# A two-layer relational graph convolution with a layer norm: batches of three 14-tile chunks instead of single 10-tile chunks, on one core

## The chip, the cores and the metric

One core of a Trainium2 chip (trn2) runs the whole kernel. The metric is device time in microseconds (us) of one execution; the time given for a kernel is the median of several runs. One more execution is taken by the hardware profiler, and all rows, timelines and waits below are of that one. Engines are named as the profile names them: PE is TensorE, PEld its weight load, ACT is ScalarE, DVE is VectorE, POOL is GpSimd, SP is SyncE.

## The reference

There are 50,000 nodes with 128 features, 850,000 edges sorted by their destination, 16 relations and 8 bases. A layer sums the sources of all edges per destination and relation, multiplies by the relation's matrix (a mix of the bases), adds the node's own product and a bias, and applies a relu. Two layers follow each other, and the input plus the second layer's output is normalised.

```python
W = jnp.einsum('rb,bio->rio', w_comp, basis)
seg = dst.astype(jnp.int32) * N_REL + rel.astype(jnp.int32)
agg = jax.ops.segment_sum(h[src], seg, num_segments=N_ENT * N_REL)
agg = agg.reshape(N_ENT, N_REL, -1)
msg = jnp.einsum('nri,rio->no', agg, W)
out = jax.nn.relu(msg + h @ loop_w + bias)
...
h = layer(x, basis1, w_comp1, loop_w1, bias1)
h = layer(h, basis2, w_comp2, loop_w2, bias2)
return _layernorm(x + h, axis=-1)
```

## The kernel before

Edges are cut into tiles of 128, one edge per partition: 6,641 tiles in each layer. As edges are sorted by destination, a tile's edges belong to a few neighbouring nodes: the kernel allows 12 (WN). It first reads all destinations and builds, for the whole graph, the source indices `src`, the node of each edge within its tile (`key`), and the place of each tile's 12 slots within a window of 128 nodes (`slot`, `base_i`, `dist`); a flag read at the end of this phase chooses `chunked` or a slower way, `summed`, which doesn't run here.

`chunked` walks over chunks of 10 tiles (K), 665 per layer. For each tile, POOL gathers the 128 source rows by an indirect DMA (L156, called at L437) into one of six buffers of 10 tiles (`rows`). SP loads the chunk's 128-node window of the layer's input (`hw`), in layer 2 also of x (`xw`). Every fourth chunk `weights` (L347 to L374) turns the relations of 40 tiles into each edge's 8 basis weights `pm`: a compare on DVE (L364) and five matmuls (L367). DVE makes `own` (L442), which says which of the 12 slots an edge belongs to, and `hot` (L449), its product with the 8 weights. Then PE makes one matmul per tile (pa, L460): the gathered rows are the stationary operand and `hot` the moving one, 96 columns wide, so pa holds 8 x 12 sums per feature. ACT copies five tiles' sums at a time to `aT` (L467).

The rest of a chunk, `finish`, is done one chunk later. `slots` (L376) multiplies `aT` by the 8 bases in 8 matmuls (ps, L380) with `aT` stationary and the basis moving, 128 columns; ACT copies the result (L384). `nodes_of` (L387) sends the 120 slots to the window's nodes by a matmul with a 0/1 matrix `own` (pn, L394) and adds the part that belongs to this window from the chunk before, shifted (L397, L398); `kept` hands the sum on (L400). The window's own rows are transposed (`turned`, L163, copied by ACT at L165) and multiplied by `loop_w` (po, L402), the bias is added (L404, L405), and `ended` (L408) applies the relu and stores (layer 1, L411 and L412), or adds x, normalises (`normed`, L317 to L331, the last step on ACT at L330) and stores to the output.

The Tile framework orders each engine's instructions and gives them semaphores. Gathers signal eight shared semaphores in turn, so that each gather waits for the one eight before it; each also waits for the pa matmul that read its place in the buffers 60 tiles before. Each pa matmul waits for its own gather's semaphore. Tile is free to interleave pa matmuls with ps matmuls of the chunk before, and does.

Layer 2's gathers read layer 1's output H, so they begin only when all stores to it have landed.

## Time and profile before

| what | value |
|---|---|
| median of 3 runs | 19,358.97 us (19,357.04 to 19,359.93) |
| the profiled execution | 19,372.98 us, its span 19,371.2 us |
| POOL busy | 12,549.9 us in 13,290 instructions, 13,282 of them gathers |
| PE busy | 10,651.0 us in 60,630 records (an fp32 matmul leaves two) |
| DVE, ACT busy | 4,042.3 us, 3,098.8 us |
| DMA, mean busy share | 0.24 in the middle of layer 1, 0.25 in that of layer 2 |
| granted PE clock, mean | 0.711 |
| pause of the gathers between the layers | 46.26 us |

A row of the profile's groups reads: line, engine, operation, tile written <- tiles read, shape, count | busy us in total, mean ns of one | idle us of the engine just before them, and what ended most of it. "remote" and "another core or an unknown queue" stand for a wait whose releaser the trace doesn't name; this kernel has one core, so it is something of its own. "issue" means that nothing visible was waited for. A timeline row reads: start, duration, engine, line, operation, tiles, and in brackets the idle time before it and what ended it.

### The profile page before, as it was taken

To read this page: it belongs to the slowest core of one execution; us is meant where nothing else is said; L and a number is where in the kernel's file an instruction comes from. 1 tells how busy PE (TensorE), PEld (TensorE's weight loads), DVE (VectorE), ACT (ScalarE), POOL (GpSimd) and SP (SyncE) were. 2 spreads that over 40 slices of the span, in tenths; PEclk is the share of its full clock that TensorE was granted. 3 is DMA by queue.
4 is the path that set the end of the run, shared out by engine and by line. 5 is a ranking of instruction groups with operands and counts; after the bars stand their busy time and mean duration, and the time that the engine had idled before them with its cause. 6 is when DMAs were issued, how large, how long until landed. Compare 5 with 4: busy or idle time off the path is not lost.

```text
span 19371.2 us, 191086 instructions
## 1 busy us (share of the span) xinstructions
PE 10651.0 (55%) x60630; PEld 10113.3 (52%) x60630; DVE 4042.3 (21%) x11719; ACT 3098.8 (16%) x8680; POOL 12549.9 (65%) x13290
## 2 busy tenths in 40 slices
PE   4555555555555555555545555555555555555555
PEld 4555555555555555555545555555455555555555
DVE  2111111111111111111212222222222222222222
ACT  1111111111111111111111111111111111111111
POOL 6666666666666666666566666666666666666665
PEclk6767777777766777767767777777777777777777
DMA  2222222222222222222222222222222222222222
GB/s 74 61 61 61 61 61 60 61 61 60 61 61 60 61 61 61 60 60 61 57 62 65 65 65 65 65 66 65 65 65 65 65 66 65 65 65 65 65 66 58
DMA packets 961778, 1218.82 MB, mean 63 GB/s; under 512 B 275684, under 2 KB 704100, under 8 KB 960768
## 3 DMA queue, kind: packets, MB, share of 16 engines
q0 software_dynamic: 425024, 871.30, 18.2%
q1 hardware_dynamic: 525876, 333.73, 5.8%
q8 instruction: 493, 8.08, 0.2%
q14 instruction: 517, 4.24, 0.1%
q10 hardware_dynamic: 9868, 1.48, 0.1%
HBM read 1118.27 MB, written 87.16 MB: 62 GB/s over the span
## 4 chain that ended last, share of the span: by engine, by line
another core or an unknown queue 41%; PE 32%; issue 15%; ACT 6%; DVE 3%; POOL 1%; DMA 1%; ACTq 0%; POOLq 0%; DVEq 0%; SPq 0%
PE pa L460 12%; PE ps L380 9%; PE pn L394 4%; PE pn L398 2%; PE po L402 2%; ACT aT L467 2%; PE pm L367 2%; ACT o L330 1%; PE po L163 1%; POOL g L156 1%; ACT slots L384 1%; ACT sd L324 1%; DVE s L404 1%; DVE t L415 1%
## 5 line engine op out<-in xcount | busy, mean ns | idle before, releaser
L156 POOL DMA_INDIRECT g<-H,src x6641 | 6268.2, 944 | 3412.4 <-issue 1309.9
L156 POOL DMA_INDIRECT g<-in_x_dram,src x6641 | 6280.8, 946 | 3358.2 <-issue 1297.4
L460 PE MATMUL pa<-hot,g 128*128 128x96 f32 x26564 | 5855.6, 334 | 65.3 <-issue 43.5
L380 PE MATMUL ps<-basis,aT 128*120 128x128 f32 x21280 | 4983.0, 363 | 1245.5 <-issue 706.2
L460 PEld LDWEIGHTS pa<-hot,g 128*128 128x128 f32 x26564 | 5414.9, 265 | 72.1 <-issue 48.3
L380 PEld LDWEIGHTS ps<-basis,aT 128*120 128x120 f32 x21280 | 4068.7, 258 | 1383.2 <-issue 788.2
L394 PE MATMUL pn<-slots,own 120*128 120x128 f32 x2660 | 885.1, 428 | 6010.0 <-ACT slots L384 4923.0
L394 PEld LDWEIGHTS pn<-slots,own 120*128 120x128 f32 x2660 | 560.1, 262 | 6213.6 <-ACT slots L384 5071.8
L467 ACT COPY aT<-pa 128x480 f32<-128x480 f32 x2658 | 1483.5, 558 | 10051.8 <-remote 7007.2
L390 DVE TENSOR_SCALAR own<-fixed,slot 120x128 f32<-120x128 f32 x1330 | 466.6, 351 | 12561.5 <-PE pn L394 7454.3
L449 DVE TENSOR_TENSOR hot<-pm,own 128x960 f32<-128x960 f32 x1330 | 1535.2, 1155 | 1685.4 <-remote 880.2
L402 PE MATMUL po<-loop,hT 128*128 128x128 f32 x2660 | 831.7, 407 | 597.4 <-ACT hT L165 255.9
L402 PEld LDWEIGHTS po<-loop,hT 128*128 128x128 f32 x2660 | 567.9, 266 | 728.8 <-issue 339.4
L163 PE MATMUL po<-ident,hw 128*128 128x128 f32 x1330 | 510.6, 384 | 744.4 <-DVE s L404 369.4
L400 ACT COPY kept<-pn 128x128 f32<-128x128 f32 x1330 | 352.7, 265 | 2780.0 <-remote 1118.2
L163 PEld LDWEIGHTS po<-ident,hw 128*128 128x128 f32 x1330 | 310.9, 234 | 794.7 <-DVE s L404 399.9
L398 PE MATMUL pn<-kept,shift 128*128 128x128 f32 x2656 | 718.0, 365 | 0.0
L367 PE MATMUL pm<-each,is_rel 128*128 128x64 f32 x3340 | 656.1, 324 | 15.5 <-issue 15.4
L367 PEld LDWEIGHTS pm<-each,is_rel 128*128 128x128 f32 x3340 | 617.5, 253 | 14.1 <-issue 14.0
L398 PEld LDWEIGHTS pn<-kept,shift 128*128 128x128 f32 x2656 | 601.7, 278 | 0.2
L384 ACT COPY slots<-ps 120x128 f32<-120x128 f32 x1330 | 349.6, 263 | 1301.2 <-remote 1117.6
L397 DVE TENSOR_SCALAR shift<-fixed,dist 128x128 f32<-128x128 f32 x1328 | 461.9, 348 | 331.0 <-remote 182.4
(78 smaller groups left out, 3233.1 us busy)
## 6 DMA issues: line engine op xcount, KB each, us to landing
g<-in_x_dram,src POOLq DMA_INDIRECT x6641
g<-H,src POOLq DMA_INDIRECT x6641
rel<-in_edges_dram SPq DMA_DIRECT2D x332, 320.0 KB
hw<-in_x_dram SPq DMA_DIRECT2D x665, 64.0 KB
H<-h SPq DMA_DIRECT2D x665, 64.0 KB
hw<-H SPq DMA_DIRECT2D x665, 64.0 KB
xw<-in_x_dram SPq DMA_DIRECT2D x665, 64.0 KB
out_dram<-o SPq DMA_DIRECT2D x665, 64.0 KB
```

The lines of the kernel that those rows point to most:

```text
L156: nc.gpsimd.indirect_dma_start(out=to, out_offset=None, in_=of, in_offset=bass.IndirectOffsetOnAxis(ap=idx, axis=0))
L163: nc.tensor.transpose(tp[:, :m], h, ident[:m, :m])
L367: nc.tensor.matmul(pm[:, :, j * NB : (j + 1) * NB], is_rel[:, j * P : (j + 1) * P], EACH[n], start=True, stop=True,)
L380: nc.tensor.matmul(ps[: k * WN], aT[:, b, : k * WN], BASIS[n][:, b, :], start=b == 0, stop=b == NB - 1)
L384: nc.scalar.copy(st[: k * WN], ps[: k * WN])
L390: nc.vector.tensor_scalar(own[: k * WN], grid[: k * WN, :P], slot[: k * WN, c : c + 1], None, op0=OP.is_equal)
L394: nc.tensor.matmul(pn, own[: k * WN], st[: k * WN], start=True, stop=not c)
L398: nc.tensor.matmul(pn, shift, kept, start=False, stop=True)
L402: nc.tensor.matmul(po, turned(hw, P, sb), LOOP[n], start=True, stop=True)
L449: nc.vector.tensor_tensor(hot[:, :ks], pm[:, t0 : t0 + ks, :, None].to_broadcast([P, ks, NB, WN]), own[:, :ks, None, :].to_broadcast([P, k ...
L460: nc.tensor.matmul(pa[:, i * NB * WN : (i + 1) * NB * WN], g[:, k + i, :], hot[:, k + i].rearrange("e b w -> e (b w)"), start=True, stop=True,
L467: nc.scalar.copy(aT[:, :, k * WN : (k + m) * WN].rearrange("d b (i w) -> d i b w", w=WN), pa[:, : m * NB * WN].rearrange("d (i b w) -> d i ...
```

## The change

A chunk has 14 tiles (475 per layer) and a batch has three chunks, 42 tiles; the last four batches of each layer have one chunk each, so a layer has 161 batches. There are seven row buffers of 14 tiles, 98 in all. The order of instructions is written by hand (`manual_schedule`): after each group of five pa matmuls and its ACT copy, one of the five steps of the batch before is issued. The steps are `bases_products` (the bases are now stationary and up to 504 slots of `aT` move), `turned_back` (six transposes bring the slots back onto partitions, with DVE's 0/1 matrices for the batch in one compare), `nodes_turned` (the three windows' transposes), `nodes_products` and `ended`. A chunk's window is arranged so that its first tile also carries over the slots of the tile before it, and the handing on by `kept` and `shift` remains only in the last three chunks. The bias enters as one more row of the matmul.

Each row buffer has a semaphore of its own. The gathers of a chunk, issued from its last tile to its first, all add to it; the chunk's first pa matmul waits for the sum, and the others wait for nothing. Tile gives these gathers no semaphore.

In layer 2 the last step of the normalisation is three VectorE instructions instead of an ACT one per chunk. The preparing phase builds the places of two halves of seven tiles and a few more conditions on them, and `key` is bfloat16. `weights` makes six matmuls of 56 columns on 112 partitions, once per batch. PSUM pools: two buffers for pa, one each for ps, transposes, pn and pm.

```diff
-K = P // WN
-S = K * WN
+K = 14
+M = 3
+HALF = K // 2
+S = (HALF + 1) * WN
 BATCH = 8
-AT = 8
-PER = 5
-GATHERS = 6
+AT = 7
+PER = 6
+GROUP = 5
+GATHERS = 7
...
+    SUMS = [[consts.tile([P, 2 * M, D], F32, name=f"sums{n}_{i}") for i in range(2)] for n in range(2)]
+    OWN = [consts.tile([P, 2 * M, P], F32, name=f"own{i}") for i in range(2)]
+    for n, bias in enumerate((bias1, bias2)):
+        for sums in SUMS[n]:
+            nc.scalar.dma_start(
+                sums[S : S + 1].rearrange("p (m a) d -> p a m d", a=2)[:, 0],
+                bass.AP(tensor=bias.tensor, offset=bias.offset, ap=[[D, 1], [0, M], [1, D]]),
+            )
+    for own in OWN:
+        nc.vector.memset(own[S : S + 1], 1.0)
...
     ps_a = ctx.enter_context(tc.tile_pool(name="ps_a", bufs=2, space=PSUM))
-    ps_o = ctx.enter_context(tc.tile_pool(name="ps_o", bufs=1, space=PSUM))
+    ps_s = ctx.enter_context(tc.tile_pool(name="ps_s", bufs=1, space=PSUM))
+    ps_t = ctx.enter_context(tc.tile_pool(name="ps_t", bufs=1, space=PSUM))
     ps_n = ctx.enter_context(tc.tile_pool(name="ps_n", bufs=1, space=PSUM))
-    ps_m = ctx.enter_context(tc.tile_pool(name="ps_m", bufs=2, space=PSUM))
+    ps_m = ctx.enter_context(tc.tile_pool(name="ps_m", bufs=1, space=PSUM))
...
+        landed = [tc.alloc_semaphore(f"landed{i}") for i in range(GATHERS)]
+        counts = [0] * GATHERS
+        def flat(of):
+            return of.bitcast(U8).rearrange("n d -> (n d)")
+        def window(of, n0):
+            return flat(of)[ds(n0, P * D * 4)].rearrange("(p d) -> p d", p=P)
+        with (
+            tc.tile_pool(name="once", bufs=1) as once,
+            tc.tile_pool(name="twice", bufs=2) as twice,
+            tc.manual_schedule(),
...
+            sizes = [M] * ((C - 4) // M) + [1 + (C - 4) % M] + [1] * 3
+            n_done = len(sizes)
...
+                def load(self):
+                    self.n0 = bases(self.c0, self.m)
+                    self.hw = twice.tile([P, M, D], F32, name="hw")
+                    self.xw = twice.tile([P, M, D], F32, name="xw") if self.n else None
+                    for j in range(self.m):
+                        nc.sync.dma_start(self.hw.bitcast(U8)[:, j, :], window(self.of, self.n0[j]))
+                    for j in range(self.m if self.n else 0):
+                        nc.sync.dma_start(self.xw.bitcast(U8)[:, j, :], window(x, self.n0[j]))
...
+                def fetch(self, j):
+                    c, k = self.c0 + j, self.chunk_tiles(j)
+                    at = (self.n * C + c) % GATHERS
+                    g = rows[at]
+                    if self.n == 0 and c < n_first:
+                        return g, None, None
+                    counts[at] += 16 * k
+                    count, name = counts[at], f"rows{self.n}_{c}"
+                    for t in reversed(range(k)):
+                        one = gather(g[:, t, :], self.of, src[:, c * K + t : c * K + t + 1])
+                        one.then_inc(landed[at], 16)
+                        tc.no_tile_sem_insts.add(one.ins.name)
+                        tc.add_to_no_dep_group(name, one.ins)
+                    def others(inst):
+                        tc.declare_no_dep(inst.ins, group=name, reason="the first reader has waited for all rows")
+                    def first(inst):
+                        inst.wait_op(landed[at], count, "sem-ge")
+                        tc.declare_no_dep(inst.ins, group=name, reason="waits for all of the rows itself")
+                        tc.declare_fence(inst.ins, group=name)
+                    return g, first, others
...
+                    def bases_products():
+                        ps = ps_s.tile([P, BANK], F32, name="ps")
+                        for b in range(NB):
                             nc.tensor.matmul(
+                                ps[:, :slots], BASIS[n][:, b, :], self.aT[:, b, :slots], start=b == 0, stop=b == NB - 1
                             )
+                        if before is None:
+                            nc.vector.memset(sT[:, :WN], 0.0)
+                        else:
+                            nc.scalar.copy(sT[:, :WN], before.sT[:, before.tiles * WN : (before.tiles + 1) * WN])
+                        nc.scalar.copy(sT[:, WN : WN + slots], ps[:, :slots])
+                    def turned_back():
+                        nc.vector.tensor_tensor(
+                            own[:S, : 2 * m, :],
+                            grid[:S, None, :].to_broadcast([S, 2 * m, P]),
+                            slot[:S, c0 : c0 + m, :].rearrange("s c a -> s (c a)")[:, :, None].to_broadcast(
+                                [S, 2 * m, P]
+                            ),
+                            op=OP.is_equal,
                         )
+                        pt = ps_t.tile([P, 2 * M, P], F32, name="pt")
+                        for at, s0, k in parts:
+                            nc.tensor.transpose(pt[:k, at, :], sT[:, s0 : s0 + k], ident)
+                        if whole:
+                            nc.scalar.copy(sums[:S, : 2 * m, :], pt[:S, : 2 * m, :])
+                        else:
+                            for at, s0, k in parts:
+                                nc.scalar.copy(sums[:k, at, :], pt[:k, at, :])
+                    def nodes_turned():
+                        pt = ps_s.tile([P, BANK], F32, name="ps")
+                        for j in range(m):
+                            nc.tensor.transpose(pt[:, j * P : (j + 1) * P], self.hw[:, j, :], ident)
+                        self.hT = twice.tile([P, M * P], F32, name="hT")
+                        nc.scalar.copy(self.hT[:, : m * P], pt[:, : m * P])
+                    def nodes_products():
+                        self.pn = ps_n.tile([P, M, D], F32, name="pn")
+                        self.kept = None
+                        for j in range(m):
+                            c = c0 + j
+                            pn = self.pn[:, j, :]
+                            alone = c >= C - 3
+                            mine = [p for p in parts if p[0] // 2 == j]
+                            for at, s0, k in mine:
+                                if at == 2 * j and not alone:
+                                    k += 1
+                                nc.tensor.matmul(
+                                    pn,
+                                    own[:k, at, :],
+                                    sums[:k, at, :],
+                                    start=at == 2 * j,
+                                    stop=alone and at == mine[-1][0] and c == C - 3,
+                                )
+                            if not alone:
+                                nc.tensor.matmul(
+                                    pn, self.hT[:, j * P : (j + 1) * P], LOOP[n], start=False, stop=True
+                                )
+                                continue
...
+                    def ended():
+                        if n == 0:
+                            o = twice.tile([P, M, D], F32, name="o")
+                            nc.scalar.activation(o[:, :m, :], self.pn[:, :m, :], AF.Relu)
+                        else:
+                            t = twice.tile([P, M, D], F32, name="t")
+                            nc.vector.scalar_tensor_tensor(
+                                t[:, :m, :], self.pn[:, :m, :], 0.0, self.xw[:, :m, :], op0=OP.max, op1=OP.add
+                            )
...
+                            o = twice.tile([P, M, D], F32, name="o")
+                            for j in range(m):
+                                nc.vector.tensor_scalar(
+                                    o[:, j, :],
+                                    t[:, j, :],
+                                    mv[:, j, 0:1],
+                                    rs[:, j : j + 1],
+                                    op0=OP.subtract,
+                                    op1=OP.mult,
+                                )
+                        for j in range(m):
+                            nc.sync.dma_start(window((H1, out)[n], self.n0[j]), o.bitcast(U8)[:, j, :])
+                    return [bases_products, turned_back, nodes_turned, nodes_products, ended]
...
+            handed = [[], []]
+            batches = [Batch(n, i) for n in range(2) for i in range(n_done)]
+            batches[0].load_rel()
+            batches[0].compare()
+            batches[0].weights()
+            hot = batches[0].weighted(0)
+            steps = []
+            for q, batch in enumerate(batches):
+                later = batches[q + 1] if q + 1 < len(batches) else None
+                batch.load()
+                if later is not None:
+                    later.load_rel()
+                batch.aT = aT = twice.tile([P, NB, M * K * WN], F32, name="aT")
+                for t0 in range(0, batch.tiles, GROUP):
+                    pa = ps_a.tile([P, BANK], F32, name="pa")
+                    m = min(GROUP, batch.tiles - t0)
+                    for t in range(t0, t0 + m):
+                        j, k = divmod(t, K)
+                        if k == 0:
+                            hot_j = hot
+                            g, first, others = batch.fetch(j)
+                            if j == batch.m - 1 and later is not None:
+                                later.compare()
+                            if j < batch.m - 1:
+                                hot = batch.weighted(j + 1)
+                        one = nc.tensor.matmul(
+                            pa[:, (t - t0) * NB * WN : (t - t0 + 1) * NB * WN],
+                            g[:, k, :],
+                            hot_j[:, k].rearrange("e b w -> e (b w)"),
+                            start=True,
+                            stop=True,
+                        )
+                        if first is not None:
+                            (others if k else first)(one)
+                    nc.scalar.copy(
+                        aT[:, :, t0 * WN : (t0 + m) * WN].rearrange("d b (i w) -> d i b w", w=WN),
+                        pa[:, : m * NB * WN].rearrange("d (i b w) -> d i b w", i=m, w=WN),
+                    )
+                    if steps:
+                        steps.pop(0)()
+                    if later is not None and t0 <= (batch.m - 1) * K < t0 + GROUP:
+                        later.weights()
+                        hot = later.weighted(0)
+                for step in steps:
+                    step()
+                steps = batch.steps(batches[q - 1] if batch.i else None)
+                if later is None or later.n != batch.n:
+                    for step in steps:
+                        step()
+                    steps = []
```

## The prediction

> **What bounds the kernel now.** I read the busy shares first, then the row of the gathers, then what the gathers wait for, then the timelines of GpSimd (POOL), ScalarE (ACT) and TensorE (PE).
>
> ```profile
> PE 10651.0 (55%) x60630; PEld 10113.3 (52%) x60630; DVE 4042.3 (21%) x11719; ACT 3098.8 (16%) x8680; POOL 12549.9 (65%) x13290
> another core or an unknown queue 41%; PE 32%; issue 15%; ACT 6%; DVE 3%; POOL 1%; DMA 1%; ACTq 0%; POOLq 0%; DVEq 0%; SPq 0%
> L156 POOL DMA_INDIRECT g<-H,src x6641 | 6268.2, 944 | 3412.4 <-issue 1309.9
> L156 POOL DMA_INDIRECT g<-in_x_dram,src x6641 | 6280.8, 946 | 3358.2 <-issue 1297.4
> L380 PE MATMUL ps<-basis,aT 128*120 128x128 f32 x21280 | 4983.0, 363 | 1245.5 <-issue 706.2
> L394 PE MATMUL pn<-slots,own 120*128 120x128 f32 x2660 | 885.1, 428 | 6010.0 <-ACT slots L384 4923.0
> L467 ACT COPY aT<-pa 128x480 f32<-128x480 f32 x2658 | 1483.5, 558 | 10051.8 <-remote 7007.2
> ```
>
> No engine is full. POOL is nearest, and its idle 6770.6 us is of two kinds. The timeline shows them: 0.30 us after each gather, which nothing removes, and pauses.
>
> ```profile
> 28.50 0.94 POOL L156 DMA_INDIRECT g<-in_x_dram,src  x1 [0.30 <-issue]
> 29.75 0.94 POOL L156 DMA_INDIRECT g<-in_x_dram,src  x1 [0.30 <-issue]
> ...
> 5010.40 0.94 POOL L156 DMA_INDIRECT g<-in_x_dram,src  x1 [0.30 <-issue]
> 5011.65 0.94 POOL L156 DMA_INDIRECT g<-in_x_dram,src  x1 [0.30 <-issue]
> 5014.85 0.94 POOL L156 DMA_INDIRECT g<-in_x_dram,src  x1 [2.26 <-PE pn L398]
> ...
> 9639.59 0.94 POOL L156 DMA_INDIRECT g<-in_x_dram,src  x1 [0.30 <-issue]
> 9686.80 0.94 POOL L156 DMA_INDIRECT g<-H,src  x1 [46.26 <-DMA H<-h]
> ```
>
> Layer 2's first gathers run from 9686.80 to a start at 9779.17 without a pause: 74 steps in 92.37 us, **1.248 us a gather**. All 13,282 need 13,282 x 1.248 = 16,579 us; the other 2,790 us of the span are pauses, in which a gather waits for a row buffer, that is for the pa matmul of 60 tiles before. The gathers thus lead by six full buffers, and it is the consumers that are late. Here is why, in one chunk:
>
> ```profile
> 5006.43 0.36 PE L460 MATMUL pa<-hot,g 128*128 128x96 f32 x2
> 5006.63 0.41 PE L402 MATMUL po<-loop,hT 128*128 128x128 f32 x2
> 5013.53 0.80 PE L394 MATMUL pn<-slots,own 120*128 120x128 f32 x2 [6.49 <-ACT slots L384]
> ```
>
> ```profile
> 5011.14 0.56 ACT L467 COPY aT<-pa 128x480 f32<-128x480 f32 x1 [7.72 <-remote]
> 5013.22 0.27 ACT L384 COPY slots<-ps 120x128 f32<-120x128 f32 x1 [1.52 <-remote]
> ```
>
> The last ps and pa matmuls are recorded as over by 5007, yet the copies that need them start at 5011.14 and 5013.22: PE's result reaches ACT 4 to 6 us late, and PE stands for 6.49 us. Set side by side over the span, copies start after their last recorded matmul by 2.9 us on average for aT (quartiles 0.0 and 5.2) and 4.9 us for slots (1.4 and 7.5). In the drain after layer 1's last gather the lags are mostly 0.04 to 0.3 us, and pn starts at 9657.76, 9662.95, 9668.48: 5.4 us a chunk, against 19,371 / 1,330 = 14.6. So PE's work is not the limit; its late hand-offs while gathers are in flight are. What delays them, the records don't say; I can only count what goes with them: before, nearly every pa matmul waits on its own gather, and about every PE instruction signals.
>
> **What the Trainium skill says.** "DMA: Bandwidth & Descriptors", section on why a DMA increments its semaphore by 16: only a full count means landed, and each in-flight slot wants its own semaphore. That is what the change builds, with the full count of a chunk; no run yet shows its time. The same page's anatomy of a SWDGE DMA gives about 2.0 us fixed; here a gather's last semaphore write comes 2.21 us (median) after its start, so latency is far below the lead of 60 gathers (60 x 1.248 = 75 us). "Perfetto Trace Analysis", summary of profiler windows: TensorE's recorded end is estimated, and SWDGE's end is the descriptors', not the data's. The trace agrees (0.94 us recorded, 2.21 us to landing), and the first half warns that part of the lag may be real PE work. "Advanced Engine Details and Errata", VectorE performance modes: two-port VectorE work blocks GpSimd. A gather at 30.99, beside such VectorE work, took 1.55 us; the mean of 0.945 shows it is rare.
>
> **The change, part by part**, per 42 tiles (one batch, or 4.2 chunks before; 13,282 / 42 = 316.2 of them).
> - **Own semaphores.** 42 PE waits on gathers become 3; each gather loses the wait for the one eight before it; POOL's wait for PE falls to about one per chunk. With groups of five pa in a row, and eight ps without pa between, I count some 20 to 25 awaited or unmerged PE signals against about 68 (21,600 recorded for 316). Price of the new wait: the first pa of a chunk waits for 14 rows, 14 x 1.248 = 17.5 us of gathers, and everything behind it on PE waits too. The seven buffers hold 98 rows, so POOL goes on meanwhile: nothing. Without that cover it is 17.5 us per chunk.
> - **Wide base products and the rest of PE.** A recorded fp32 matmul is two passes, each about (stationary + moving) columns. Before, a chunk: pa 20 x 224, ps 16 x 248, pn 2 x 256, shift, loop 2 x 256 each, turn 256, pm 2.5 x 192 = 10,720; x 4.2 = 45,000. After: pa 84 x 224 = 18,816; ps 16 x 632 = 10,112; pm 12 x 184 = 2,208; nine transposes 2,304; pn 12 x 256 and loop 6 x 256 = 4,608; total 38,050. At the drain's pace (4.2 x 5.4 = 22.7 us for 45,000) that is 19 us, at half of it 38 us. POOL's 42 gathers take 52.4 us. Both ends are hidden. The 504-column matmul is not in the trace; if it cost twice its columns, the slow end would be 48 us, still hidden.
> - **ACT and DVE.** ACT: 9 x 0.56 for aT plus five wide copies (about 3.5 us) = 8.5. DVE: three hot of 14/10 x 1.155 = 1.62, is_rel 0.55, own_w and own about 1.5, layer 2 about 3: 7 to 10 us. Beside 52.4, nothing. The normalising step moves from ACT (0.494) to three VectorE scalings; they may hold up gathers: from 0 to 966 x 0.06 = 60 us; the middle, 20, goes into the sum.
> - **SP.** Three hw, three xw, one rel, three stores per batch, one bases load: 29% fewer than before per edge. A store now stands in SP's queue ahead of the next batch's loads and waits for the end of the batch before; hw is wanted only a batch later: nothing. Without that cover, the load's latency per batch, a few us.
> - **Single chunks at the layer's end** shorten what follows the last gather. Before: 46.3 us between layers, 19,371.2 - 19,321.1 = 50 at the end. After, PE is not behind: landing 2.2, five tiles, two sets of five steps at 1.5 us, a store of 2 to 4: about 25 each (bounds 15 and 45).
>
> **Sum.** The 61st gather starts at 102.96 and POOL has hardly paused till then. The 13,221 others: 13,221 x 1.248 = 16,500. Plus 25 + 25 + 20: span 16,673; with the 1.8 us around it, 16,675 against 19,373 for the profiled execution. The median of the runs is 0.07% under that execution: **16,665 us, -13.9%**. The next limit is POOL's own 1.248, which the change leaves alone.
>
> **Rivals.** With lag L per PE-to-ACT hand-off, the hand-written order costs about 4.5 x (L + 2.7) for nine pa groups on two PSUM buffers, and 3 x (L - 2) for the dependent steps in PE's order (aT to ps, sT to transposes, sums to pn): 7.5 L + 6.2 us per batch. At today's mean L of 3 to 5 it is 28 to 44, under 52.4. The formula is my estimate.
> - **Lag stays, and at its upper values**: L = 6.5 gives 55 us; 316.2 x 55 + 83 (first pa) + 50 = 17,520. For it: the cause is unknown, and gathers will come faster. Against: fewer signals and waits.
> - **No change**: batch 61.2 us (19,371 / 316.2), L = 7.3; the change then doesn't do what its semaphores are for. About 19,370; a narrow case.
> - **Slower**: from L = 7.3 the single buffers of ps, pt and pn and PE's fixed order decide: where Tile let pa fill a wait, PE now stands. At L = 8, 66.2 us: 316.2 x 66.2 + 133 = 21,070. For it: the upper quartile of slots is 7.5 already. Against: that is a quarter of the hand-offs, and the drain shows lag falls to 0.1 when PE isn't chased by events.
>
> **Chances.** Gathers bind, 16,560 to 16,850: 0.70. Lag stays, 16,850 to 18,800: 0.22. No change: 0.02. Slower: 0.06. Faster by over 0.2% (what a measurement here can tell from none): 0.92; within: 0.02; slower: 0.06. The range takes the first case from its lower bounds, and half of the second: 16,550 to 17,600.
>
> **What would show it.** Right: gather steps of 1.25 us with hardly a pause, POOL near 75% busy, PE's idle ended by gathered rows at a chunk's first pa, a gap between layers near 25 us. Wrong: POOL pauses ended by PE pa; sT or sums copies starting 5 us or more after their matmuls; gathers above 0.95 us in layer 2 alone (VectorE); a step other than 1.25 us.

## The result and the profile after

| | before | after |
|---|---|---|
| median | 19,359.45 us (4 runs, 19,357.04 to 19,369.42) | 19,635.76 us (4 runs, 19,628.51 to 19,639.37) |
| ratio | | 1.0141 [1.0124, 1.0159] |
| span of the profiled execution | 19,371.2 us | 19,637.6 us |
| one tile, from gather to gather, mean of layer 1 / 2 | 1.448 / 1.451 us | 1.463 / 1.462 us |
| pause between the layers, gather start to gather start | 47.2 us | 90.5 us |
| last gather to the end | 51.0 us | 95.0 us |

The change is 1.4% slower, where 13.9% faster was forecast. Of the 266 us by which the spans differ, the step per tile makes 6,640 x (0.0154 + 0.0113) = 177 us, the pause between the layers 43, the end 44 and the start 2. The page after, rows that answer to those of before:

```profile
PE 8757.2 (45%) x44274; PEld 7106.8 (36%) x44274; DVE 2618.0 (13%) x3814; ACT 2194.8 (11%) x4495; POOL 12545.9 (64%) x13289
another core or an unknown queue 57%; PE 32%; ACT 6%; issue 4%; DVE 0%; DMA 0%; ACTq 0%; SPq 0%; DVEq 0%
L178 POOL DMA_INDIRECT g<-H,src x6641 | 6267.0, 944 | 3531.9 <-issue 1927.9
L178 POOL DMA_INDIRECT g<-in_x_dram,src x6641 | 6278.2, 945 | 3465.1 <-issue 1929.0
L670 PE MATMUL pa<-hot,g 128*128 128x96 f32 x26564 | 4378.7, 329 | 8670.4 <-ACT aT L679 7682.9
L679 ACT COPY aT<-pa 128x480 f32<-128x480 f32 (+1 forms) x2846 | 1489.3, 534 | 13889.5 <-remote 10328.1
```

PE, DVE and ACT have much less to do, and it bought nothing: POOL's idle time is 6,997 us in place of 6,771. PE's wait has moved mostly to one place, the last pa group of a batch, which waits for ACT, which waits for PE's own signal. In the timelines (start, duration) of one batch, PE, ACT and POOL:

```profile
4059.02 1.35 PE L670 MATMUL pa<-hot,g 128*128 128x96 f32 x10 [0.77 <-issue]
4089.22 3.30 PE L670 MATMUL pa<-hot,g 128*128 128x96 f32 x14 [28.85 <-ACT aT L679]
```

```profile
4058.41 0.56 ACT L679 COPY aT<-pa 128x480 f32<-128x480 f32 x1 [2.62 <-PE pa L670]
4088.61 1.02 ACT L679 COPY aT<-pa 128x480 f32<-128x480 f32 x2 [29.65 <-remote]
```

```profile
4082.86 0.94 POOL L178 DMA_INDIRECT g<-in_x_dram,src  x1 [0.30 <-issue]
4090.67 0.94 POOL L178 DMA_INDIRECT g<-in_x_dram,src  x1 [6.86 <-PE pa L670]
```

PE's ten records end at 4060.4, and the copies that need them start at 4088.61, 28 us later and 4.8 us after POOL's last gather ended. The lag I meant to remove has been gathered into one, and a batch takes 61.46 us (4027.15 to 4088.61), much as 42 tiles did before (60.8 to 60.9).

**Two conditions.** The experiments ran on several chips, and the kernel before took 16,660 to 16,670 us on some occasions and 19,352 to 19,605 on others; one chip showed both, at different times (16,664.7, later 19,352). So it is not a fixed property of a chip; what sets it, no run shows. It is not the granted PE clock, which was higher for the kernel before where that was slower (0.71 against 0.67 to 0.68). I call the first *free* and the second, in which both kernels were first measured, *held*. Each experiment below says which it met, by the time of the kernel before on the same occasion; nothing is compared across the two unless said.

### The profile page after: what moved, and what is told of

The parts are those of the page before. It is cut to its first block, busy times and chain, and to the rows that moved or that the text cites. A ratio compares the mean times of both kernels' runs of the same rounds, so it can differ in the third digit from the quotient of the medians.

```text
span 19637.6 us, 119572 instructions
## 1 busy us (share of the span) xinstructions
PE 8757.2 (45%) x44274; PEld 7106.8 (36%) x44274; DVE 2618.0 (13%) x3814; ACT 2194.8 (11%) x4495; POOL 12545.9 (64%) x13289
## 4 chain that ended last, share of the span: by engine, by line
another core or an unknown queue 57%; PE 32%; ACT 6%; issue 4%; DVE 0%; DMA 0%; ACTq 0%; SPq 0%; DVEq 0%
PE ps L540 12%; PE pa L670 12%; ACT aT L679 4%; PE pn L586 3%; PE pn L594 2%; PE pm L474 1%; ACT sums L562 1%; PE pt L560 1%; ACT hT L572 1%; PE ps L570 0%; ACT sd L627 0%; ACT sT L547 0%; ACT key L278 0%; DMA rel<-in_edges_dram 0%
## 5 line engine op out<-in xcount | busy, mean ns | idle before, releaser
L670 PE MATMUL pa<-hot,g 128*128 128x96 f32 x26564 | 4378.7, 329 | 8670.4 <-ACT aT L679 7682.9
L670 PEld LDWEIGHTS pa<-hot,g 128*128 128x128 f32 x26564 | 4173.3, 243 | 8945.4 <-ACT aT L679 7751.3
L487 DVE TENSOR_TENSOR hot<-pm,own_w 128x1344 f32<-128x1344 f32 x950 | 1477.4, 1555 | 16276.0 <-remote 13386.5
L679 ACT COPY aT<-pa 128x480 f32<-128x480 f32 (+1 forms) x2846 | 1489.3, 534 | 13889.5 <-remote 10328.1
L540 PE MATMUL ps<-aT,basis 128*128 128x504 f32 (+1 forms) x5152 | 2516.0, 647 | 0.3 <-issue 0.2
L540 PEld LDWEIGHTS ps<-aT,basis 128*128 128x128 f32 x5152 | 1102.0, 223 | 1205.4 <-issue 1205.0
L586 PE MATMUL pn<-sums,own 97*128 97x128 f32 (+1 forms) x3796 | 958.3, 401 | 871.1 <-ACT sums L562 600.5
L586 PEld LDWEIGHTS pn<-sums,own 97*128 97x128 f32 (+1 forms) x3796 | 825.6, 301 | 922.7 <-ACT sums L562 632.0
L594 PE MATMUL pn<-loop,hT 128*128 128x128 f32 x1888 | 642.8, 444 | 946.1 <-ACT hT L572 920.2
L474 PE MATMUL pm<-each,is_rel 112*128 112x56 f32 x3864 | 530.3, 291 | 272.1 <-DVE is_rel L458 161.3
```

The source lines that it names most:

```text
L474: nc.tensor.matmul(pm[:, :, j * NB : (j + 1) * NB], self.is_rel[: AT * NR, j * P : (j + 1) * P], EACH[self.n][: AT * NR], start=True, stop ...
L487: nc.vector.tensor_tensor(self.hot[:, :k], self.pm[:, t0 : t0 + k, :, None].to_broadcast([P, k, NB, WN]), self.own[:, t0 : t0 + k, None, : ...
L540: nc.tensor.matmul(ps[:, :slots], BASIS[n][:, b, :], self.aT[:, b, :slots], start=b == 0, stop=b == NB - 1)
L586: nc.tensor.matmul(pn, own[:k, at, :], sums[:k, at, :], start=at == 2 * j, stop=alone and at == mine[-1][0] and c == C - 3,)
L594: nc.tensor.matmul(pn, self.hT[:, j * P : (j + 1) * P], LOOP[n], start=False, stop=True)
L670: one = nc.tensor.matmul(pa[:, (t - t0) * NB * WN : (t - t0 + 1) * NB * WN], g[:, k, :], hot_j[:, k].rearrange("e b w -> e (b w)"), start= ...
```

## Experiments

Theory 1: gathers in flight hold PE back, whoever waits for whom. Theory 2, the prediction's: waits and signals between the engines make the lateness. Theory 3: PE's work is longer than its records.

**Four kernels to take the parts asunder (free, before 16,663).** Edits to the changed kernel. `v_nog`: no gathers except at the layers' ends, pa on a constant tile. `v_indep`: the gathers go to tiles nobody reads.

```diff
+                    if not real(self):
+                        for t in range(k):
+                            gather(sink[(c * K + t) % 8], self.of, src[:, c * K + t : c * K + t + 1])
+                        return g, None, None
...
-                            g[:, k, :],
+                            g[:, k, :] if real(batch) else still,
```

`v_nostep`: `steps = [batch.out_only]`, which stores the input rows. `v_paced`: `+ nc.gpsimd.memset(pad, 0.0)` after each gather.

> Leaves out nearly all gathers (only those of each layer's last five batches and the first seven chunks stay); the pa matmuls of all other batches read one constant tile, so its output is not the reference's. Theory 1, the gathers in flight hold PE back: without them PE runs at the pace seen between the layers, 22 to 27 us per batch of 42 tiles, 7.0 to 8.7 ms in all. Theory 2, late hand-offs of the hand-written order: the hand-offs stay, 45 to 61 us per batch, 14 to 19.4 ms. Theory 3, PE's real work is longer than its records: 19 ms.

> All gathers are made, but into tiles that nobody reads except in each layer's last five batches; pa reads a constant tile, so the output is not the reference's and PE and POOL wait for each other no more. Theory 1, gathers back to back hold PE back whoever waits for whom: POOL ends each layer's gathers after 8.3 ms and PE is far behind then; 20 to 23 ms. Theory 2, the waits between PE and POOL make the lateness: PE keeps up and the gathers bind, 16.6 to 16.8 ms.

> Leaves out the five steps after the pa sums (no base products, transposes, node products, relu or norm; the input rows are stored), so PE has only pa and pm. Theory 1: PE is still slowed to about 5.6 us per tile under back-to-back gathers and POOL still has to pause, but for less work: 17.3 to 18.8 ms. Theory 2: hand-offs are too few to bind, the gathers bind: 16.6 to 16.75 ms.

> A 64-column memset on GpSimd after every gather, 0.1 to 0.3 us each. Theory 1: PE gets through in the gaps, so pauses shrink as much as the gaps grow: 19.2 to 19.7 ms, or less if short gaps are as good as long ones. Theory 2: gaps add to the gathers and the hand-offs hide them: 19.6 ms, with the pauses at chunk starts shorter. Theory 3, PE work binds: 19.6 ms, unchanged.

Measured: 7,702.6, 16,760.1, 16,711.9 and 17,133.0 us. Without gathers a batch takes 20.9 us in layer 1 and 26.7 in layer 2, so theory 3 falls. The other three stand at or near the gathers' floor, as theory 2 said of the first two (for `v_paced` theories 2 and 3 had said 19.6 ms, and missed); but the kernel before stood there too, at 16,663, and that was the surprise: in this condition there was nothing to win. The memset made a step 1.28 us.

**The changed kernel again (held, before 19,373.09).**

> The changed kernel as it is, on whatever chip it gets, beside the kernel before on the same chip. In the runs just made the kernel before took 16663 us where it took 19359 us at first, so the chip or its condition decides. If the pauses belong to a condition that is absent now, both kernels are bound by their gathers: before 16660, after 16640 to 16700. If the condition is back, 19360 and 19630 again.

19,649.19 us, ratio 1.0145 [1.0128, 1.0162]: the first result repeats.

**The uncoupled and the paced kernel again (free each time).**

> The same kernel as v_indep (all gathers made, but pa reads a constant tile except in each layer's last five batches, so the output is not the reference's), for a chip on which the kernel before takes 19360 us. Theory 1, there the gathers back to back hold PE back whoever waits for whom: PE is far behind when a layer's gathers end; 20 to 23 ms. Theory 2, the waits between PE and POOL make the lateness: 16.6 to 16.8 ms. Where the kernel before takes 16660 us: 16760 as before.

> The same kernel as v_paced (a 64-column memset on GpSimd after each gather), for a chip on which the kernel before takes 19360 us. Theory 1 with PE getting through in any gap of POOL: the pauses shrink as the steps grow, 17.1 to 18.5 ms. Theory 1 with PE needing a pause of several us: 19.6 to 20 ms. Theory 2: 19.6 ms, the same hand-offs. Where the kernel before takes 16660 us: 17130 as before.

> The same kernel as v_indep (gathers made into tiles that nobody reads, pa on a constant tile except in each layer's last five batches; the output is not the reference's). So far the kernel before took 16660 us on two chips and 19370 us on another. Where it takes 19370 us: theory 1, the gathers in flight hold PE back whoever waits for whom, 20 to 23 ms; theory 2, the waits between PE and POOL make the lateness, 16.6 to 16.8 ms. Where it takes 16660 us: 16740 again.

16,735.1, 17,132.2 and, as the median of four, 16,735.9 us against 16,665.3 (1.0042 [1.0022, 1.0062]). They tell nothing of the held condition. To see many variants under one condition, I put them into one kernel.

**Stretches in one kernel: `s_a` (free), `s_b` (held, before 19,600.44).** Each batch has a mode:

```diff
+            MODES = ([(20, 'real'), (50, 'apart'), (75, 'paced'), (161, 'real')], [(15, 'real'), (40, 'none'), (65, 'sums only'), (90, 'pairs'), (115, 'apart half'), (140, 'apart plain'), (161, 'real')])
```

> The changed kernel in stretches of 15 to 96 batches, so that one execution holds several trials. Layer 1: batches 0 to 19 as changed; 20 to 49 gathers into tiles nobody reads and pa on a constant tile; 50 to 74 a small memset after every gather; then as changed. Layer 2: 15 as changed; 25 without gathers; 25 with pa and pm alone; 25 with one pa matmul of 192 columns for two tiles; 25 with 64-row gathers that nobody reads; 25 with plain 128-row loads by GpSimd in place of gathers; then as changed. Much of the output is therefore not the reference's. Where the kernel before takes 19370 us: theory 1 (gathers in flight hold PE back) gives, per batch of 42 tiles, 61.5 us as changed, PE well below one batch per 61 us in the stretch without coupling while POOL goes at 1.25 us per gather, about 24 us without gathers, some 55 to 58 with pa and pm alone, less than 61 for pairs if instructions are held and 61 if columns are. Theory 2 (the waits between PE and POOL) gives PE at 24 to 30 us per batch in the stretch without coupling. Where the kernel before takes 16660 us, all stretches with gathers go at 52.5 us per batch.

> The same kernel in stretches as s_a, which ran where the kernel before took 16660 us and showed 52 to 53 us per batch as changed and without coupling, 27.0 without gathers and 48.9 with pa and pm alone. Where the kernel before takes 19370 us: theory 1, gathers in flight hold PE back, gives 61.5 us per batch as changed, far over 27 for PE in the stretch without coupling, 27 without gathers. Theory 2, the waits between PE and POOL, gives 27 to 30 without coupling. Where the kernel before takes 16660 us: as s_a.

15,238.0 us (free) and 19,034.2 (held). The second decided between theories 1 and 2. Windows of `s_b` (duration, then busy us and count of PE, its weight loads, DVE, ACT, POOL, granted clock, DMA share, GB/s): as changed, uncoupled (gathers into tiles nobody reads, pa on a constant tile) while the gathers stream, uncoupled after they had ended:

```profile
700.00:1200.00 500.00, 218.93 (x1112) 176.80 (x1112) 53.23 (x48) 54.62 (x112) 321.04 (x340) 0.66 0.22 57
2500.00:2700.00 200.00, 26.64 (x93) 19.82 (x92) 4.80 (x5) 4.18 (x8) 154.77 (x144) 0.53 0.18 47
3200.00:3400.00 200.00, 197.98 (x1329) 160.46 (x1329) 63.85 (x57) 65.94 (x134) 0.00 (x0) 1.00 0.13 38
```

The same instructions, with nothing to wait for from POOL: 93 records in 200 us while gathers stream, 1,329 when they don't. From the ACT copies that begin each batch, the two whole batches on the constant tile while they stream take 389.3 and 389.2 us (as do the two before them, whose rows had long been gathered), and one takes 20.9 when they don't. In `v_indep`, free, PE went at 20.9 us a batch with the gathers streaming:

```profile
200.00:2900.00 2700.00, 2673.88 (x18010) 2172.50 (x18009) 860.70 (x777) 902.36 (x1814) 2049.20 (x2136) 1.00 0.34 88
```

Theory 2 is dead: there is no wait to blame. It is no lack of data either: with 64-row gathers that nobody reads a batch again took 389.3 us, while beside plain 128-row loads issued by POOL every 0.53 us it took 27. It is also not PE's work that sets the pace when coupled: steady batches took 62.0 us as changed, 61.5 (median; mean 60.0) with pa and pm alone, 62.1 (median; mean 63.4) with half the pa weight loads, 62.1 paced. Theory 1 had expected 55 to 58 for pa and pm alone, so it is no account of the coupled batch as it stands.

**The changed kernel beside it (held, before 19,600.44).**

> The changed kernel again. Where the kernel before takes 16660 us both are bound by the gathers at 1.25 us each: 16640 to 16720, the layer change at 30 us instead of the before's, the end 20 us shorter; theory 1 and 2 say the same here. Where the kernel before takes 19370 us: 19640 again.

19,807.89 us, ratio 1.0107 [1.0091, 1.0124]; the kernel before had not been 19,600 elsewhere.

**Semaphores, batch size, buffers and rests: `s_c` (free, before 16,663.37), `s_d` (held, before 19,364.38).** The edits: Tile's semaphores (`gather` alone, and `return g, None, None`), fewer row buffers (`% 4`, `% 2`), 1024-column memsets among the gathers, and single-chunk batches.

> The changed kernel with 100 batches of three chunks and then 175 of one chunk per layer, in stretches. Layer 1: batches 0 to 19 as changed; 20 to 39 with Tile's semaphores, each pa waiting on its own gather; 40 to 59 four row buffers in place of seven; 60 to 79 one 1024-column memset on GpSimd after every 7 gathers; 80 to 99 two after every 14; then single chunks, first with the own semaphores and then with Tile's. Layer 2: as changed; four memsets after every 42; two after every 7; two row buffers; as changed; single chunks on four buffers; single chunks. Where the kernel before takes 19370 us: if PE is held by streaming gathers alone, neither the semaphores nor the size of a batch nor the number of buffers matters, and all stretches without memsets lie at 60.5 to 63 us per 42 tiles; rests that PE can use make the pauses vanish: 52.4 plus the rests, 57 to 60 us, if a rest of about 1 us frees PE, and the rests on top of 61.5 if not. If Tile's waits or the long batch cost the 1.4%, those stretches differ by 0.6 us or more. Where the kernel before takes 16660 us: 52.5 us, and the rests on top where they are not hidden.

> The same kernel in stretches as s_c, which ran where the kernel before took 16660 us and showed 52.0 to 53.3 us per 42 tiles in every stretch without memsets or with more than two buffers, and 56 to 64 with memsets. Where the kernel before takes 19370 to 19600 us: if PE is held by streaming gathers alone, the stretches without memsets lie at 60.5 to 63 us whatever their semaphores, batch and buffers; with memsets 57 to 60 if short rests free PE, 66 to 73 if not. If Tile's waits or the long batch make the 1.4%, those stretches differ from the own semaphores by 0.6 us or more.

17,330.8 and 19,806.0 us. Steady us per 42 tiles, from the ACT copies that begin the batches (the first of each stretch left out), for single chunks from the steps of the gathers:

| stretch | free | held |
|---|---|---|
| as changed, layer 1 / 2 | 52.5 / 52.5 | 61.4 / 61.5 |
| Tile's semaphores | 52.5 | 59.9 |
| four buffers / two buffers | 52.5 / 53.2 | 61.4 / 61.4 |
| one memset after every 7 | 57.5 | 60.7 |
| two after every 14 | 58.0 | 60.9 |
| four after every 42 | 56.4 | 61.5 |
| two after every 7 | 63.6 | 63.7 |
| single chunks, own / Tile's semaphores | 52.7 / 52.7 | 61.1 / 60.8 |

Rests that cost 4 to 5.5 us free cost nothing held, where 57 to 60 or 66 to 73 us had been expected: they only take the place of pauses. Two buffers do as well as seven. So the pauses are not the cause of the 61.4 us. A rate of the gathers' own would fit; `s_g`, below, tests it.

**The changed kernel, free (before 16,663.37).**

> The changed kernel, for a chip on which the kernel before takes 16660 us: both are bound by 13282 gathers at 1.25 us, so 16640 to 16720 us. Where the kernel before takes 19370 us: 19640 again.

16,710.49 us, ratio 1.0028 [1.0017, 1.0039]. Its page, and what POOL waited for:

```profile
POOL 75%; issue 24%; PE 1%; DMA 0%; DVE 0%; ACT 0%; ACTq 0%; SPq 0%; DVEq 0%; POOLq 0%
L178 POOL DMA_INDIRECT g<-in_x_dram,src x6641 | 6287.8, 947 | 2050.3 <-issue 2022.8
L178 POOL DMA_INDIRECT g<-H,src x6641 | 6278.7, 945 | 2056.3 <-issue 2023.1
```

```profile
POOL g L178 <- issue: 4045.9, 13275, 0.3
POOL g L178 <- DMA H<-o: 32.6, 1, 32.6
POOL g L178 <- ACT src L278: 26.6, 1, 26.6
```

Here POOL's idle time is its 0.30 us after each gather and two waits at the layers' starts: the picture that I forecast.

**Without the own semaphores (free, before 16,664.80), and gathers alone (free).** `v_lanes` is the changed kernel with Tile's semaphores; in `s_e` some batches make only gathers and store zeros.

> The whole changed kernel, but with Tile's semaphores for the gathers as before (each pa waits on its own gather, gathers in ascending order). Where PE is held (before 19370 us): 59.9 us per 42 tiles as in that stretch of s_d, against 61.4 with the own semaphores: 316 x 59.9 + 320 = 19.2 to 19.3 ms, a little faster than before and 1.5 to 2.5% faster than the change. Where it is not held (before 16660 us): bound by the gathers, 16700 to 16780 us.

> The changed kernel with stretches in which only the gathers are made, into tiles nobody reads, and zeros are stored; PE, ACT and DVE do nothing: layer 1 batches 20 to 49 with 128 rows, 70 to 99 with 32 rows; layer 2 batches 20 to 49 with 128 rows. The output is not the reference's. Where the kernel before takes 19370 us: if a gather itself can be kept up only at 1.40 us there, the step goes from 1.25 to 1.40 us after some 235 gathers, with PE idle too, and with 32 rows as well; if it was the contention with PE, it stays at 1.25 us. Where the kernel before takes 16660 us: 1.25 us throughout.

16,723.04 us (1.0034 [1.0022, 1.0047]) and 16,605.21. Gathers alone went at 1.249 us, with 32 rows at 1.167. No version was found that beats both kernels: free, the kernel before is already near the floor; held, where 19.2 to 19.3 ms were expected of `v_lanes`, it was never measured.

**Gathers alone and Tile's semaphores: `s_f` (free), `s_g` (held, before 19,352.06), the same kernel.**

```diff
+                if batch.mode > 0:
...
+                    for j in range(batch.m):
+                        batch.fetch(j)
...
+                    continue
```

> The changed kernel, in layer 1 with a stretch (batches 20 to 49) in which only gathers are made, into tiles nobody reads, and zeros are stored (so the output is not the reference's), in layer 2 with Tile's semaphores for batches 0 to 79 and the own ones after. Where the kernel before takes 19370 us: if a gather itself can be kept up only at 1.40 us there, its step goes from 1.25 to 1.40 us after some 235 gathers with PE idle too; if contention with PE made it, it stays at 1.25. Batches with Tile's semaphores 59.9 us, with the own ones 61.4. Where the kernel before takes 16660 us: 1.25 us throughout and 52.5 us per batch.

> The same kernel as s_f, which fell where the kernel before took 16660 us and took 16722. Where the kernel before takes 19370 us: a step of 1.40 us with PE idle, after some 235 gathers, if a gather itself can be kept up only at that rate, 1.25 if contention with PE made it; batches with Tile's semaphores 59.9 us against 61.4 with the own ones.

16,722.4 and 19,448.9 us. Two windows of `s_g` after PE's last held-up work was over, the first with stores of zeros beside the gathers, the second with nothing but gathers; below them one of `s_f`, free:

```profile
2200.00:2500.00 300.00, 0.00 (x0) 0.00 (x0) 0.00 (x0) 0.49 (x1) 234.12 (x215) 0.50 0.24 67
2600.00:2900.00 300.00, 0.00 (x0) 0.00 (x0) 0.00 (x0) 0.00 (x0) 234.73 (x215) 0.50 0.17 47
```

```profile
1700.00:2000.00 300.00, 0.00 (x0) 0.00 (x0) 0.00 (x0) 0.00 (x0) 226.66 (x241) 0.50 0.20 53
```

The gathers start 1.400 us apart (median) in both held windows, and 1.248 in the free one. PE did nothing in any, so contention with PE does not make the step. POOL's timeline of `s_g` where the step changes, after 180 gathers without a pause (235 expected; the last 152 of them in that stretch):

```profile
1442.25 0.94 POOL L178 DMA_INDIRECT sink<-in_x_dram,src  x1 [0.30 <-issue]
1443.50 0.95 POOL L178 DMA_INDIRECT sink<-in_x_dram,src  x1 [0.30 <-issue]
1444.75 0.98 POOL L178 DMA_INDIRECT sink<-in_x_dram,src  x1 [0.30 <-issue]
1446.03 1.09 POOL L178 DMA_INDIRECT sink<-in_x_dram,src  x1 [0.30 <-issue]
1447.43 1.09 POOL L178 DMA_INDIRECT sink<-in_x_dram,src  x1 [0.30 <-issue]
```

The duration goes from 0.94 to 1.09 us and the step from 1.25 to 1.40. In layer 2 Tile's semaphores gave 59.9 us per batch over 68 batches, the own ones 61.5 over 65, as expected.

## Why the prediction was wrong

**The step that failed** is the first: "1.248 us a gather. All 13,282 need 13,282 x 1.248 = 16,579 us; the other 2,790 us of the span are pauses", and with it "The next limit is POOL's own 1.248". I took the step of 74 gathers without a pause for a rate that can be kept up. In the held condition it can't: gathers run at 1.25 us for 180 in a row (179 in `s_b`), then at 1.40, with PE idle too (`s_g`). It looks as if something between can hold that much in store. Then 42 tiles cost 42 x 1.400 = 58.8 us, and only 1.1 (Tile's semaphores) to 2.6 us (own) of the batch are left for everything else. That this rate sets the coupled batch too is argued, from this sum and from the rests that cost nothing; no coupled stretch ran long enough without a pause to show the 1.40 itself. The trace of before could not show it either, as its longest run without a pause had 75 gathers. Its pauses fit in the main: ten gathers at 1.25 fall 10 x 0.15 = 1.5 us behind 1.40, and its 1,774 pauses of over 0.5 us, 1.48 us in the mean, make 2.0 us per ten gathers.

**Cause and symptom were exchanged.** "It is the consumers that are late" described the waits rightly and the cause wrongly. As I now read the runs: while more gathers are given out than are kept up with, PE gets on at a crawl, 389 us a batch, and recovers when POOL pauses. POOL then seems to wait for PE, which really waits for the gathers' remainder. Hence the numbers that didn't move: fewer signals, fewer waits, fewer PE records (44,274 in place of 60,630), rests, two buffers. What the remainder consists of is open: rows landed 2.14 us (median) after the start of their gather in the held changed kernel, and 2.20 in the free one, so it isn't the rows; and it doesn't depend on their number (64 rows: 1.40 too).

**One time of 0.70 us, and a rival.** SP's register moves, under 0.05 us in the free condition, took about 0.70 us 32% of the time in the held changed kernel, so not PE alone is slowed. The same time comes back elsewhere: the held gather step of 1.40 us is twice 0.70, and PE beside streaming gathers often goes one matmul (with its weight load) per 2.80 us, four times 0.70. In `s_g`:

```profile
1856.63 0.32 PE L699 MATMUL pa<-hot,g 128*128 128x96 f32 x1 [2.08 <-issue]
1859.43 0.32 PE L699 MATMUL pa<-hot,g 128*128 128x96 f32 x1 [2.48 <-issue]
1862.23 0.32 PE L699 MATMUL pa<-hot,g 128*128 128x96 f32 x1 [2.48 <-issue]
```

A batch has 139 such records, and 139 x 2.80 = 389.2 us is the batch of `s_b`. The held traces also lack records of semaphore updates, which fits with the many releasers in them that are "remote" or "an unknown queue" (41% and 57% of the chain before and after, none in `g_after`): the changed kernel left 63,266 such records held and 267,075 free. With gathers alone there were 3,840 for 240 gathers free (`s_f`, 2200 to 2500), 16 each, and held 430 for 214 (`s_g`, the same window), two each, one per 0.70 us. So POOL, PE and SP seem to share something that moves once in 0.70 us. It may be the recording itself, so that the held time is in part that of being recorded; no run here separates the two. Against a recorder too slow for everything: beside the plain loads in `s_b` 17,532 updates were recorded in 500 us (16600 to 17100) and PE kept its 27 us a batch.

**The rest of the sum** can be tested where nothing is held, `g_after`, which took 16,707.2 us of span against the 16,673 worked out. The 61st gather started at 115.7, not at 102.96 (a slip of mine: in the trace of before that is the 56th, and the 61st starts at 109.19); the steps were 1.2497 and 1.2502, 16,524 us with the lengthening in them (16,520 in the sum); the pause between the layers was 33.6 and the end 33.7 us (25 each). The 20 us for the normalising step rested on a wrong count, 966 scalings where layer 2 has 475, and cost next to nothing: a gather took 945 ns in layer 2 and 947 in layer 1. PE's batch, priced at 19 to 38 us, took 20.9 in layer 1 and 26.7 in layer 2 without gathers (`v_nog`). So the parts said to be hidden were hidden: a batch's PE, ACT, DVE and SP work, the wait for 14 rows, the wide products. That 16,710 lies near the forecast 16,665 is no success, as the gain was to come from pauses: the kernel before was, by its time, free of most of them too, and 47 us faster, so there the change gives 0.28% away. Where those 47 us go, no run shows, as there is no profile of the kernel before in that condition.

**The rivals.** "Slower" came true with another mechanism. Single PSUM buffers and PE's fixed order don't decide: with any of the shorter rests, or with single-chunk batches, the held batch stays at 60.7 to 61.5 us, and without streaming gathers the same order ran at 20.9. "No change, batch 61.2 us" had the right size for a reason that isn't the right one, and got 0.02. My formula 7.5 L + 6.2 is worthless: L isn't a constant of a hand-off; it goes with the gathers (389 us a batch beside them, 20.9 without).

**Why slower, held.** `s_d` and `s_g` show two effects in opposite directions: batches of three with Tile's semaphores take 59.9 us per 42 tiles, less than the kernel before's 60.8 to 60.9 (42 x 1.448 and 1.451), and the own semaphores add 1.6. The net is +0.6 us, 177 us over the run. The own semaphores also come with gathers from the last tile to the first, and no run parts the two. Why they cost that with batches of three and at most 0.3 us with single chunks stays open. The drains make 87 us more. My 25 us each supposed that PE isn't behind; held, it was behind by up to seven buffers, 98 tiles instead of 60, when a layer's gathers ended:

```profile
9743.65 0.94 POOL L178 DMA_INDIRECT g<-in_x_dram,src  x1 [0.30 <-issue]
9834.14 0.94 POOL L178 DMA_INDIRECT g<-H,src  x1 [89.55 <-DMA H<-o]
```

That the 98 tiles in place of 60 make the drains longer is argued, not tried.

**Latency and records.** What the Trainium skill says in "DMA: Bandwidth & Descriptors" (anatomy of one DMA), about 2 us fixed for a GpSimd DMA, held in both conditions (2.14 to 2.21 us). As the page "Perfetto Trace Analysis" warns, in its summary of profiler windows, that PE's recorded end is an estimate, I noted that part of the lag might be real work; the stretch without gathers (20.9 to 27 us a batch) shows that it was not.

## What to carry to other kernels

A step seen in a burst is not a rate: before an engine's shortest step is multiplied by a count, look for the longest stretch that ran at it, or make one. When an engine waits for another that itself looks idle, and its results come late only while a third is busy, take work off the second in an experiment before concluding that its work or its waits are the bound. Look first at how many waits the trace can name: "an unknown queue" at 41% of the chain was a sign in the trace of before that the named part was not the whole. A rest put where the pauses are tells at once: if it costs nothing, the pauses are not the cause.

## What the runs showed of the hardware

An indirect gather of 128 rows had a step of 1.25 us in a burst and 1.400 us when kept up in the held condition, against 1.249 in the free one. In the held condition, back-to-back gathers slowed PE from 20.9 to 389.3 us for the same batch, one matmul per 2.80 us, and plain POOL loads at 0.53 us didn't; with gathers alone the trace kept two records of semaphore updates for each in place of 16. The same chip was found in both conditions, and the time of the kernel before differed by 16% between them.
